# Moving preparations across stages of a graph-attention and feed-forward kernel

## The chip, the cores and the metric

The kernel runs on one core of a Trainium2 chip. The metric is the device time of one execution in microseconds (us), given as the median over several runs. The engines are PE (matrix multiply), DVE (vector), ACT (activation), POOL (GpSimd) and SP (which here only issues DMAs).

## The reference

`x` has 4096 rows of 256; `adj` is a 4096 x 4096 matrix of 0 and 1. Two layers run one after the other, each with an attention part and a feed-forward part, and each part is added to its input after a layer normalisation:

```python
x = x + gat4(layernorm(x), adj, W, a1, a2)           # 4 heads of 64
x = x + scan30(layernorm(x), ln_w, ln_b, W, b)       # 30 steps, below
x = x + gat4(gat4(layernorm(x), adj, W1, a1), adj, W2, a2)
x = x + top2_of_6_experts(layernorm(x))              # three products for each expert

def gat4(x, adj, W, a):                              # for each head
    h = x @ W; f1 = h @ a_src; f2 = h @ a_dst
    e = where(adj > 0, leaky_relu(f1[:, None] + f2[None, :], 0.2), -9e15)
    return elu(softmax(e) @ h)

def step(h):                                         # repeated 30 times
    h = h + 0.01 * tanh(h)
    h = h * sigmoid(h)
    h = layernorm(h) * ln_w + ln_b
    return h @ W.T + b
```

## The kernel before, in words

The rows are cut into 32 tiles of 128, and four tiles are a row group of 512; there are eight groups. Three attentions follow one another in the program, called g0 (first layer), g1 and g2 (second layer), with the feed-forward scan between g0 and g1 and the experts (routing and products, the last stage) after g2.

**An attention** has a front and a loop. The front goes over the eight row groups with two groups of lead: it loads rows, takes their layer statistics (`over_std`, L100 to L105, the last step a power on POOL), multiplies them with the weights and fills `vals` (the values, split in two parts of fp16) and the score columns. In g0 the front also begins to turn `adj` into packed masks (`make_piece`), which g1 and g2 load ready-made. The weight tensor of an attention has eight further columns, the products of W with the attention vectors; `make` computes them (products L148, reductions L149) and, where a layer normalisation precedes, subtracts the column means (PE L155, DVE L157), so that the normalisation needs no mean later. Before, the front of g0 makes the weights of all three attentions: its own at g == 0, those of g1 and g2 at g == 3 and g == 5 from the list `late`. All their loads stand at the start on ACT's DMA queue.

The loop has 128 units: four chunks of eight row tiles, in each the four heads, in each eight units of four column tiles. A unit is 64 matmuls into `acc` (L519). They are fed by four comparisons of scores for each unit (`st`: ACT L461 or DVE L459) and two DVE mask operations for each unit (`st` L567, `below` L573). At the end of a head the sums are closed while the next head runs: ACT copies the lower part (`lo`, L468), DVE adds it (`whole_sums`, L472, twice, which is also what frees `acc`), then come L482, L486, L489, a reciprocal, the product `o` (L494), on ACT the exponential `e` (L497), and in `finish` two more DVE operations (L622, L623) and the store (L624). The rows to be added, `old`, are loaded in `begin` (L615). `u`, one buffer, holds the sums; `e` has a tile of its own. After the last head, the closing has nothing beside it.

**The feed-forward scan** runs 30 steps over eight groups, 240 slots, in an order written out by hand (`slot`, under `manual_schedule`) with each slot holding stages of several groups: tanh (ACT L832) and the addition on POOL (L833) of group `at`; silu (ACT L821), its fp16 copy (L823) and a transposing DMA of group `at-2`; the transposes on PE (`tp`, L797) and their copy (`zT`, ACT L852) of `at-3`; the products (`po`, L869 and L872) of `at-4`; the result (`y`, DVE L805) of `at-5`. Each engine works in the order in which its instructions were issued. In the first slots the x1 rows of a group are also loaded, measured (bn_stats L676), rated (L684 to L688, with a power on POOL) and normalised (`init`, four ACT operations L695). POOL's addition waits by an explicit dependency for the last DVE instruction of the same slot[...].

Ahead of the slots stands the preparation of the scan's weights, L703 to L772: W transposed and multiplied by ln_w, its mean subtracted, a power-of-two scale derived from its size (`far`, `bits`, `scale`, `inv`), then `wT` and the fp16 pair `w16`. Loads of four groups of x1 stand on POOL's queue (`load(g, nc.gpsimd)`, L92).

**Buffers.** Row groups and pieces of adj are loaded into pools opened and closed by stage (`stream`). `numbers` (L961 to L963) fills constant tables by iota on POOL ahead of the last stage's routing.

Everything outside the hand-ordered slots is ordered by a scheduler from the program order and the dependencies.

Of the kernel before, what the change touches and what calls it, by code (L numbers as in the profile page):

```python
# [11 lines left out]
F32 = mybir.dt.float32  # L12
# [11 lines left out]
P = 128  # L24
# [22 lines left out]
def gnn_ffn_kernel(ctx: ExitStack, tc: tile.TileContext, a: dict, out: bass.AP):  # L47
# [19 lines left out]
    ones = const.tile([2 * H, P], F32, name="ones")  # L67
    nc.gpsimd.memset(ones, 1.0)
# [19 lines left out]
    stream = []  # L88

    def load_ahead(src, g, view=rows_of, queue=nc.sync):  # L90
        t = stream[-1].tile([P, G, C], F32, name="rows")
        queue.dma_start(t, view(src, g))  # L92
        ahead[g] = t
# [33 lines left out]
    def weights(tag, W, a_src, a_dst, norm):  # L127
# [4 lines left out]
        def load(pool):  # L132
            for k in range(KC):
                nc.scalar.dma_start(
                    w[:, k, :C].rearrange("p (h o) -> p h o", h=H),
                    W[:, k * P : (k + 1) * P, :].rearrange("h p o -> p h o"),
                )
            ab = pool.tile([P, 2, H, D], F32, name=f"{tag}_ab")
            nc.scalar.dma_start(ab[:, 0], bcast_rows(a_src))
            nc.scalar.dma_start(ab[:, 1], bcast_rows(a_dst))  # L140
            return ab

        def make(pool, small_ps, ab):
            prod = pool.tile([P, 2, H, D], F32, name="prod")
            for k in range(KC):
                wk = w[:, k, :C].rearrange("p (h o) -> p h o", h=H)
                for s in range(2):
                    nc.vector.tensor_tensor(prod[:, s], wk, ab[:, s], OP.mult)  # L148
                nc.vector.tensor_reduce(  # L149
                    w[:, k, C:].rearrange("p (s h) -> p s h", s=2), prod, axis=AX.X, op=OP.add  # L150
                )
            if norm:
                pt = small_ps()[:, : C + 2 * H]
                for k in range(KC):
                    nc.tensor.matmul(pt, mean, w[:, k, :], start=(k == 0), stop=(k == KC - 1))  # L155
                for k in range(KC):
                    nc.vector.tensor_tensor(w[:, k, :], w[:, k, :], pt, OP.subtract)  # L157

        return w, (load, make)

    def attention(tag, src, norm, w, others, chunks, first, ends, following):
# [7 lines left out]
        with ExitStack() as scope:  # L169
            lay = scope.enter_context(tc.tile_pool(name=f"{tag}_lay", bufs=1))  # L170
            vals = lay.tile([P, NT, H, 2, 2, DV], F16, name="vals")
            r = lay.tile([P, NT, H], F32, name="r")
            nf2 = lay.tile([P, NT, H], F32, name="nf2")
            hs = lay.tile([P, 1, H, DV], F32, name="hs")
            mask = [scope.enter_context(tc.tile_pool(name=f"{tag}_mask", bufs=4))]
# [20 lines left out]
            def load_piece(n):  # L196
# [3 lines left out]
                arow[n] = stream[-1].tile([P, 2, 8 * P], I32, name="adj")  # L200
# [32 lines left out]
            with ExitStack() as ps:  # L233
# [44 lines left out]
                def greatest():  # L278
# [8 lines left out]
                    nc.vector.tensor_scalar(dm, ident[: 2 * H, : 2 * H], fx, None, op0=OP.mult)  # L287
                    pt = small_ps()
                    nc.tensor.matmul(pt[:, : 2 * H], ones, dm, start=True, stop=True)
# [107 lines left out]
                late = [functools.partial(make, prep, small_ps, get(prep)) for get, make in others]  # L397
                for g in range(NG + 2):
# [10 lines left out]
                    if g == 0 and late:  # L409
                        late.pop(0)()  # L410
# [7 lines left out]
                    if g in (3, 5) and late:  # L418
                        late.pop(0)()
# [56 lines left out]
            def close(c, h, u):  # L476
# [17 lines left out]
                nc.vector.tensor_tensor(o[:, :nt], v[:, :nt, :D], z[:, :nt].to_broadcast([P, nt, D]), OP.mult)  # L494
                yield
                e = end.tile([P, CM, D], F32, name="e")
# [40 lines left out]
            with tc.manual_schedule(engines={mybir.EngineType.DVE, mybir.EngineType.Activation}):  # L537
# [3 lines left out]
                for at in range(len(units) + LAG):  # L541
# [43 lines left out]
                    if first:  # L585
# [8 lines left out]
                        if at == len(units) - 30:  # L594
                            store_mask(len(chunks) * PER // 4 - 1)
                    if following and at == len(units) - 2 * following[0]:
# [9 lines left out]
    def to_rows(dst, src=None):  # L606
# [5 lines left out]
        def begin(t, n, h, work):  # L612
            if src is not None:
                old = work.tile([P, 8, D], F32, name="old")
# [14 lines left out]
    w0, make = weights("g0", a["L0_gnn_W"], a["L0_gnn_a1"], a["L0_gnn_a2"], True)  # L629
    gw, makers = [], []  # L630
    for n in range(2):
        av = a[f"L1_gnn_a{n + 1}"]
        for got, to in zip(weights(f"g{n + 1}", a[f"L1_gnn_W{n + 1}"], av[:, :D], av[:, D:], not n), (gw, makers)):
            to.append(got)
    with tc.tile_pool(name="adj", bufs=2) as adjacency:
        stream.append(adjacency)
        attention("g0", x, True, w0, [make, *makers], [8, 8, 8, 8], True, to_rows(x1d, x), [])
    stream.append(ctx.enter_context(tc.tile_pool(name="stream", bufs=4)))

    with ExitStack() as scope:
        one = scope.enter_context(tc.tile_pool(name="f_one", bufs=1))
        wT = one.tile([P, C], F32, name="wT")  # L650
        w16 = one.tile([P, 2, C], F16, name="w16")
        scale = one.tile([P, 2], F32, name="scale")
        under = one.tile([P, 2, G], F32, name="under")
        eps = one.tile([P, 2], F32, name="eps")
        nc.gpsimd.memset(eps[:, :1], EPS)
        nc.gpsimd.memset(eps[:, 1:], EPS * 1e-4)
        bias = one.tile([P, C], F32, name="bias")
        last = one.tile([P, C], F32, name="last")
# [4 lines left out]
        x1 = {}  # L663

        def load(g, queue=nc.sync):
            if g not in ahead:
                load_ahead(x1d, g, queue=queue)
            x1[g] = ahead.pop(g)

        measured, rates = {}, {}  # L670

        def measure(g):
            st = small.tile([P, G, 6], F32, name="x_st")
# [708 lines left out]
```

## Time and profile before

| | us |
|---|---|
| median of three runs | 2999.38 (2998.97 to 3000.24) |
| the profiled execution | 3003.1 |
| its span | 3001.4 |
| g0: front, loop | to about 98, to 603.5 |
| feed-forward | to about 1578.6 |
| g1: front, loop | to 1645, to about 2126.6 |
| g2: front, loop | to about 2196, to about 2676.4 |
| routing and experts | to the end |

The profiled execution is one of its own, 3.7 us above the median of the others; its span is 1.7 us shorter than its time, which is what lies around the first and the last instruction. Over the span PE is busy 94%, DVE 91%, ACT 82% and POOL 39%; the clock granted to PE was 0.974 of full speed on average. Busy shares are averages over stages: each stage is read by itself.

### The profile page before, as it was taken

The numbers are of one execution on the slowest core, as the hardware profiler recorded it, in microseconds if no ns is written. First come the engines' busy times: TensorE is split into PE (matmuls) and PEld (weight loads), VectorE is DVE, ScalarE is ACT, GpSimd is POOL, SyncE is SP. The second block draws the span as 40 slices with busy tenths as digits, with TensorE's granted clock in tenths as the row PEclk, the third lists the DMA queues.
The fourth block names the chain that finished last, engine by engine and source line by source line (L and its number), as shares of the span: only waits on it lengthen the run. The fifth ranks groups of instructions, "written<-read, shape, count | busy, mean of one in ns | idle before, by whom it ended". The sixth has DMA issues, their size and how long they took to land. (4 is left out here: it accounts for less than half of the span.)

```text
span 3001.4 us, 82666 instructions
## 1 busy us (share of the span) xinstructions
PE 2812.5 (94%) x33923; PEld 2569.1 (86%) x33923; DVE 2737.4 (91%) x5766; ACT 2469.0 (82%) x3132; POOL 1161.5 (39%) x1080
## 2 busy tenths in 40 slices
PE   6899999969999999999998999999889999986996
PEld 5799999958888888888886999999789999975996
DVE  7999999989999999999998899999689999986775
ACT  5799999888888888888876999999699999963342
POOL 2000000079999999999982000000200000013663
PEclk9999999989999999999999999999999999997998
DMA  9998884153333333333353031221303132133253
GB/s 286 270 252 242 232 234 141 29 134 68 68 68 68 70 69 68 68 68 68 68 110 114 20 104 54 73 79 27 107 20 93 51 107 79 51 100 119 82 173 134
DMA packets 482899, 320.08 MB, mean 107 GB/s; under 512 B 416573, under 2 KB 443354, under 8 KB 476378
## 3 DMA queue, kind: packets, MB, share of 16 engines
q1 hardware_dynamic: 467698, 287.13, 35.8%
q0 software_dynamic: 7680, 21.51, 2.3%
q10 hardware_dynamic: 7144, 6.16, 0.7%
q8 instruction: 268, 4.39, 0.6%
q14 instruction: 109, 0.89, 0.1%
HBM read 183.00 MB, written 52.04 MB: 78 GB/s over the span
## 5 line engine op out<-in xcount | busy, mean ns | idle before, releaser
L519 PE MATMUL acc<-vals,st 128*128 128x130 f16 x12288 | 1434.6, 219 | 36.1 <-DVE u L472 27.5
L519 PE MATMUL acc<-vals,below 128*128 128x130 f16 x12288 | 1434.2, 221 | 12.4 <-DVE below L573 11.9
L461 ACT ACTIVATE st<-f1b,nf 128x1024 int8<-128x1024 f32 x1265 | 1334.6, 1143 | 32.7 <-PE acc L519 23.6
L519 PEld LDWEIGHTS <-below 128*128 128x128 fp8e4 x12288 | 1177.6, 96 | 48.8 <-issue 43.8
L519 PEld LDWEIGHTS <-st 128*128 128x128 fp8e4 x12288 | 1209.3, 98 | 10.0 <-DVE st L567 7.5
L869 PE MATMUL po<-wT,zT 128*128 128x256 f32 x1920 | 574.8, 381 | 4.7 <-ACT zT L852 3.4
L872 PE MATMUL po<-w,zT 128*128 128x256 f16 x3840 | 576.8, 273 | 0.0
L833 POOL TENSOR_TENSOR th<-th,y 128x1024 f32<-128x1024 f32 x240 | 567.2, 2363 | 21.7 <-ACT th L832 4.4
L872 PEld LDWEIGHTS <-zT 128*128 128x128 f16 x3840 | 376.2, 98 | 160.1 <-issue 0.6
L573 DVE TENSOR_TENSOR below<-m,st 128x1024 int32<-128x1024 int32 x384 | 470.0, 1224 | 32.7 <-DVE st L567 1.3
L567 DVE TENSOR_TENSOR st<-st,m 128x1024 int32<-128x1024 int32 x384 | 467.5, 1217 | 1.1 <-ACT st L461 0.9
L805 DVE SCALAR_TENSOR_TENSOR y<-po,z_rs,bias 128x256 f32<-128x256 f32 x928 | 384.5, 477 | 2.1 <-PE tp L797 0.7
L845 DVE BATCH_NORM_STATS2 z_st<-z 128x6 f32<-128x256 f32 x960 | 335.9, 413 | 0.0
L869 PEld LDWEIGHTS po<-wT,zT 128*128 128x128 f32 x1920 | 290.4, 191 | 14.0 <-ACT zT L852 5.8
L821 ACT ACTIVATE z<-th 128x1024 f32<-128x1024 f32 x240 | 251.8, 1049 | 15.2 <-POOL th L833 14.9
L105 POOL TENSOR_TENSOR ln_rstd<-ln_rstd,mhalf 128x4 f32<-128x4 f32 x24 | 31.7, 1321 | 590.9 <-ACT acc L1035 491.8
L832 ACT ACTIVATE th<-y 128x1024 f32<-128x1024 f32 x240 | 250.1, 1042 | 0.1
L856 POOL TENSOR_TENSOR z_rs<-z_rs,mhalf 128x4 f32<-128x4 f32 x240 | 244.1, 1017 | 3.1 <-ACT z_rs L855 3.1
L852 ACT COPY zT<-tp 128x512 f32<-128x512 f32 x240 | 140.5, 585 | 90.8 <-PE tp L797 89.5
L459 DVE TENSOR_SCALAR st<-f1b,nf 128x1024 int8<-128x1024 f32 x271 | 201.2, 743 | 7.7 <-PE acc L519 7.7
L436 POOL MEMSET hs<- 128x4 f32 x3 | 0.3, 101 | 497.7 <-DVE u L489 491.1
L824 DVE SCALAR_TENSOR_TENSOR z<-z,scale,z 128x512 f16<-128x512 f32 x240 | 178.4, 743 | 4.9 <-ACT z L823 4.9
(253 smaller groups left out, 2961.2 us busy)
## 6 DMA issues: line engine op xcount, KB each, us to landing
adj<-in_adj_dram SPq DMA_DIRECT2D x64, 1024.0 KB
m<-edges SPq DMA_DIRECT2D x32, 1024.0 KB
f1b<-fd SPq DMA_DIRECT2D x48, 512.0 KB
edges<-m SPq DMA_DIRECT2D x16, 1024.0 KB
y<-yd SPq DMA_DIRECT2D x16, 512.0 KB
ew<-in_L_ffn_expert_w_dram SPq DMA_DIRECT2D x18, 256.0 KB
t<-in_x_dram SPq DMA_DIRECT2D x8, 512.0 KB
old<-in_x_dram SPq DMA_DIRECT2D x16, 256.0 KB
```

The lines of the kernel that those rows point to most:

```text
L461: nc.scalar.activation(out, f1, AF.Sign, bias=f2, scale=-1.0)
L519: nc.tensor.matmul(acc[:, i, cols], masked[part][:, at_i // TR, s, rows], v[:, cols], start=(j == 0 and part == 0), stop=(j == NT - 1 and ...
L567: nc.vector.tensor_tensor(above, above, whole, OP.bitwise_and)
L573: nc.vector.tensor_tensor(below, whole, above, OP.bitwise_xor)
L805: nc.vector.scalar_tensor_tensor(t[:, r, :] if end else y[:, g * G + r, :], po[:, r, :], rstd[:, r : r + 1], t[:, r, :] if end else bias, ...
L821: nc.scalar.activation(z, th.pop(u), AF.Silu, scale=0.01)
L832: nc.scalar.activation(th[at], y[:, g * G : (g + 1) * G, :], AF.Tanh, scale=0.01)
L833: ins = nc.gpsimd.tensor_tensor(th[at], th[at], y[:, g * G : (g + 1) * G, :], OP.add)
L845: nc.vector.bn_stats(st[:, r, :], z[:, r, :])
L856: nc.gpsimd.tensor_tensor(rs[u], rs[u], mhalf, OP.pow)
L869: nc.tensor.matmul(po[:, r, :], src[:, r * P : (r + 1) * P], wT, start=True, stop=False)
L872: nc.tensor.matmul(po[:, r, :], src16[:, part * G + r, :], w16[:, other, :], start=False, stop=(part == 1 and other == 1),)
```

## The change

The scan's weights are made in g0's front, at g == 2, instead of after its loop; some of the operations go from DVE to ACT or POOL. The products of g1's weights go into g0's last chunk and those of g2's into g1's last chunk, at units counted from the end (`side`); the subtraction of the mean (`centre`) of g1's goes to the start of g1's front. The first four groups of x1 are loaded by SP and measured in g0's last chunk, and rated there; `init` normalises in place, one slot earlier. Groups 4 to 7 get tiles of their own. Input rows and pieces of adj share one ring of four buffers for the whole kernel. `e` is written into the half of `u` that is no longer needed; `old` shares the two buffers of `lo`. The iota of the large table is cut in four with one shared integer buffer. The first POOL addition of the scan waits for `o` of the last head. The diff, cut to its core:

```diff
+    closed = []
+    ring = keep.tile([P, 4, G, C], F32, name="ring")
+    turns = [0]
 
     def load_ahead(src, g, view=rows_of, queue=nc.sync):
-        t = stream[-1].tile([P, G, C], F32, name="rows")
+        t = ring[:, turns[0] % 4]
+        turns[0] += 1
...
-        def load(pool):
+        def load(space, queue):
+            ab = space[:, : 2 * C].rearrange("p (s h d) -> p s h d", s=2, h=H)
             for k in range(KC):
-                nc.scalar.dma_start(
+                queue.dma_start(
                     w[:, k, :C].rearrange("p (h o) -> p h o", h=H),
                     W[:, k * P : (k + 1) * P, :].rearrange("h p o -> p h o"),
                 )
-            ab = pool.tile([P, 2, H, D], F32, name=f"{tag}_ab")
-            nc.scalar.dma_start(ab[:, 0], bcast_rows(a_src))
-            nc.scalar.dma_start(ab[:, 1], bcast_rows(a_dst))
-            return ab
-
-        def make(pool, small_ps, ab):
-            prod = pool.tile([P, 2, H, D], F32, name="prod")
+            queue.dma_start(ab[:, 0], bcast_rows(a_src))
+            queue.dma_start(ab[:, 1], bcast_rows(a_dst))
+
+        def make(space, k):
+            ab, prod = (
+                space[:, i * 2 * C : (i + 1) * 2 * C].rearrange("p (s h d) -> p s h d", s=2, h=H) for i in range(2)
+            )
+            wk = w[:, k, :C].rearrange("p (h o) -> p h o", h=H)
+            for s in range(2):
+                nc.vector.tensor_tensor(prod[:, s], wk, ab[:, s], OP.mult)
+            nc.vector.tensor_reduce(w[:, k, C:].rearrange("p (s h) -> p s h", s=2), prod, axis=AX.X, op=OP.add)
+
+        def centre(small_ps):
+            pt = small_ps()[:, : C + 2 * H]
             for k in range(KC):
-                wk = w[:, k, :C].rearrange("p (h o) -> p h o", h=H)
-                for s in range(2):
-                    nc.vector.tensor_tensor(prod[:, s], wk, ab[:, s], OP.mult)
-                nc.vector.tensor_reduce(
-                    w[:, k, C:].rearrange("p (s h) -> p s h", s=2), prod, axis=AX.X, op=OP.add
-                )
-            if norm:
-                pt = small_ps()[:, : C + 2 * H]
-                for k in range(KC):
-                    nc.tensor.matmul(pt, mean, w[:, k, :], start=(k == 0), stop=(k == KC - 1))
-                for k in range(KC):
-                    nc.vector.tensor_tensor(w[:, k, :], w[:, k, :], pt, OP.subtract)
-
-        return w, (load, make)
-
-    def attention(tag, src, norm, w, others, chunks, first, ends, following):
+                nc.tensor.matmul(pt, mean, w[:, k, :], start=(k == 0), stop=(k == KC - 1))
+            for k in range(KC):
+                nc.vector.tensor_tensor(w[:, k, :], w[:, k, :], pt, OP.subtract)
+
+        return w, (load, make, centre)
...
+                arow[n] = ring[:, 2 * (n % 2) : 2 * (n % 2) + 2].rearrange("p s r c -> p s (r c)").bitcast(I32)
...
-                late = [functools.partial(make, prep, small_ps, get(prep)) for get, make in others]
+                late = (front(prep, small_ps) if front else None) or []
...
-                    if g == 0 and late:
+                    if g in (0, 2) and late:
...
-                    if g in (3, 5) and late:
-                        late.pop(0)()
...
+                closed[:] = [
+                    nc.vector.tensor_tensor(o[:, :nt], v[:, :nt, :D], z[:, :nt].to_broadcast([P, nt, D]), OP.mult)
+                ]
...
-                e = end.tile([P, CM, D], F32, name="e")
+                e = u[:, :, 1, :D]
...
+                    if len(units) - at in side:
+                        side[len(units) - at]()
...
-                old = work.tile([P, 8, D], F32, name="old")
+                old = work.tile([P, 4, 2, DV], F32, name="old", tag="lo", bufs=2)
...
+    def begin_weights(n):
+        load, _, _ = layers[n][1]
+        load(ring[:, 3].rearrange("p r c -> p (r c)"), nc.sync)
+
+    def make_weights(n, k):
+        layers[n][1][1](ring[:, 3].rearrange("p r c -> p (r c)"), k)
...
+    def load_ffn():
+        ln = w16[: 2 * KC, 0, :].bitcast(F32)
+        nc.scalar.dma_start(ln[:KC], a["L0_ffn_ln_w"].rearrange("(k p) -> k p", p=P))
+        nc.scalar.dma_start(ln[KC:], a["L0_ffn_ln_b"].rearrange("(k p) -> k p", p=P))
+        wr = wT, last
+        for k in range(KC):
+            nc.scalar.dma_start(wr[k], a["L0_ffn_W"][k * P : (k + 1) * P, :])
+        nc.scalar.dma_start(bias, bcast_rows(a["L0_ffn_b"]))
+        return ln, wr
+
+    def make_ffn(prep, small_ps, loaded):
+        ln, wr = loaded
+        ps = small_ps()
+        nc.tensor.transpose(ps[:, : 2 * KC], ln, ident[: 2 * KC, : 2 * KC])
+        lnT = prep.tile([P, 2 * KC], F32, name="lnT")
+        nc.vector.tensor_scalar(lnT, ps[:, : 2 * KC], 100.0, None, op0=OP.mult)
+        ps = small_ps().rearrange("p (k c) -> p k c", k=KC)
+        for k in range(KC):
+            for o in range(KC):
+                nc.tensor.transpose(ps[:, k, o * P : (o + 1) * P], wr[o][:, k * P : (k + 1) * P], ident)
+        raw = prep.tile([P, KC, C], F32, name="raw", tag="g0_ab")
+        nc.scalar.copy(raw, ps)
...
+        nc.vector.scalar_tensor_tensor(bias, bias, 100.0, ps, op0=OP.mult, op1=OP.add)
+        nc.gpsimd.tensor_scalar(last, bias, -100.0, 0.01, op0=OP.add, op1=OP.mult)
+        for k in range(KC):
+            nc.scalar.activation(raw[:, k, :], raw[:, k, :], AF.Copy, scale=lnT[:, k : k + 1])
...
+        sq = prep.tile([P, KC, C], F32, name="sq")
+        nc.scalar.activation(sq, raw, AF.Square)
...
+        nc.gpsimd.tensor_tensor(far[:, 1:2], far[:, 0:1], mhalf[:, :1], OP.pow)
+        nc.gpsimd.tensor_tensor(far[:, 1:2], far[:, 1:2], far[:, 0:1], OP.mult)
...
+        nc.gpsimd.tensor_scalar(under[:, 1, :], under[:, 0, :], 0.01, None, op0=OP.mult)
+        nc.vector.tensor_scalar(wT, raw[:, 0, :], scale[:, :1], scale[:, 1:], op0=OP.mult, op1=OP.mult)
+        nc.scalar.activation(w16[:, 0, :], raw[:, 1, :], AF.Copy, scale=scale[:, 1:])
...
+    def init(g):
+        rs, nm = rates.pop(g)
+        for r in range(G):
+            nc.scalar.activation(
+                x1[g][:, r, :], x1[g][:, r, :], AF.Identity, scale=rs[:, r : r + 1], bias=nm[:, r : r + 1]
+            )
...
+    def front(prep, small_ps):
+        load, make, centre = layers[0][1]
+        space = prep.tile([P, 4 * C], F32, name="g0_ab")
+        load(space, nc.scalar)
+        loaded = load_ffn()
+
+        def make_first():
+            for k in range(KC):
+                make(space, k)
+            centre(small_ps)
+
+        return [make_first, lambda: make_ffn(prep, small_ps, loaded)]
+
+    side = {
+        31: [(begin_weights, 1)],
+        28: [(load, g) for g in range(3)],
+        26: [(make_weights, 1, 0)],
+        22: [(make_weights, 1, 1)],
+        20: [(load, 3)],
+        14: [(measure, 0)],
+        8: [(measure, 1)],
+        4: [(rate, 0), (rate, 1), (measure, 2)],
+        1: [(measure, 3), (init, 0), (init, 1), (rate, 2), (rate, 3)],
+    }
+    attention(
+        "g0",
+        x,
+        True,
+        w0,
+        front,
+        [8, 8, 8, 8],
+        True,
+        to_rows(x1d, x),
+        [],
+        {k: functools.partial(many, *v) for k, v in side.items()},
...
-        for g in range(4):
-            load(g, nc.gpsimd)
...
-            for g in range(3):
-                measure(g)
-                if g < 2:
-                    rate(g)
-            init(0)
...
+        hold = scope.enter_context(tc.tile_pool(name="f_hold", bufs=NG - NG // 2))
+
+        def load_apart(src, g):
+            x1[g] = hold.tile([P, G, C], F32, name="x1")
+            nc.sync.dma_start(x1[g], rows_of(src, g))
+
+        for g in range(4, NG):
+            load_apart(x1d, g)
...
-            if 0 < at and at + 3 < NG:
-                load(at + 3)
...
+                was = x1.pop(at) if at < NG else y[:, g * G : (g + 1) * G, :]
+                nc.scalar.activation(th[at], was, AF.Tanh, scale=0.01)
+                ins = nc.gpsimd.tensor_tensor(th[at], th[at], was, OP.add)
+                if not at:
+                    lower = closed[0]
...
-            if at + 2 < NG:
-                rate(at + 2)
-            if at + 1 < NG:
-                init(at + 1)
-            if at + 3 < NG:
-                measure(at + 3)
+            if 4 <= at + 3 < NG:
+                rate(at + 3)
+            if 2 <= at + 2 < NG:
+                init(at + 2)
+            if 4 <= at + 4 < NG:
+                measure(at + 4)
...
+    def centre_weights(prep, small_ps):
+        layers[1][1][2](small_ps)
...
+        for k, v in {24: (begin_weights, 2), 14: (make_weights, 2, 0), 10: (make_weights, 2, 1)}.items()
...
+            parts = 4 if math.prod(shape) > 1024 else 1
+            shape[0] //= parts
+            for i in range(parts):
+                ti = rone.tile([P, *shape], I32, name=f"{name}_i", tag="ints")
+                nc.gpsimd.iota(
+                    ti,
+                    pattern=[list(x) for x in zip([s for s, _ in pattern], shape)],
+                    base=base + i * shape[0] * pattern[0][0],
+                    channel_multiplier=step,
+                )
+                nc.gpsimd.tensor_copy(tf[:, i * shape[0] : (i + 1) * shape[0]], ti)
```

## The prediction

> **What bounds the kernel now.** I read the profile page first, then busy time by stretches, then the ACT and PE timelines where PE is idle, then the waits of the loops and the chain at the last stage. Columns of the stretches: PE, PEld, DVE, ACT, POOL busy us, granted clock, DMA share, GB/s.
>
> ```profile
> 50.00:100.00 50.00, 32.81 (x150) 25.41 (x148) 47.09 (x87) 34.58 (x53) 16.36 (x24) 0.86 0.96 298
> ...
> 540.00:600.00 60.00, 59.40 (x1028) 59.15 (x1026) 56.87 (x72) 49.98 (x51) 0.00 (x0) 1.00 0.10 23
> 600.00:610.00 10.00, 5.06 (x68) 4.50 (x66) 9.72 (x33) 2.32 (x5) 1.54 (x4) 0.93 0.23 54
> 610.00:620.00 10.00, 5.52 (x12) 2.78 (x10) 5.31 (x11) 7.23 (x14) 6.21 (x9) 0.50 0.88 263
> 620.00:630.00 10.00, 1.11 (x4) 0.71 (x4) 9.20 (x35) 8.11 (x13) 6.54 (x6) 0.50 0.53 165
> 630.00:640.00 10.00, 8.52 (x45) 6.32 (x46) 8.09 (x36) 9.94 (x20) 9.45 (x11) 0.70 0.57 157
> ...
> 650.00:750.00 100.00, 98.90 (x707) 80.75 (x706) 98.51 (x330) 89.74 (x134) 94.39 (x77) 1.00 0.41 74
> ```
>
> The reader should see three regimes: the first front is DVE's (47.09 of 50); the loop's end and the feed-forward are PE's (59.40 of 60, 98.90 of 100), with DVE only 5% behind; and from 603.5, the last attention matmul, to about 650 nothing is full. That seam is what the change attacks. On ACT's timeline it reads:
>
> ```profile
> 611.64 2.07 ACT L695 ACTIVATE y<-rows,x_nm,x_rs 128x256 f32<-128x256 f32 x4 [2.33 <-POOL x_nm L688]
> ...
> 621.38 1.28 ACT L821 ACT_TABLE_LOAD   x1
> 622.68 1.06 ACT L821 ACTIVATE z<-th 128x1024 f32<-128x1024 f32 x1
> 625.60 0.72 ACT L823 ACTIVATE z<-z,scale 128x512 f16<-128x512 f32 x1 [1.86 <-DVE inv L763]
> ```
>
> and on PE's:
>
> ```profile
> 632.59 1.22 PE L869 MATMUL po<-wT,zT 128*128 128x256 f32 x2 [1.06 <-ACT zT L852]
> ...
> 654.29 0.70 PE L869 MATMUL po<-wT,zT 128*128 128x256 f32 x2 [1.10 <-ACT zT L852]
> ```
>
> The first normalised group is ready only at 613.7, the first silu at 622.7, its fp16 copy waits for the weights' scale until 625.6, the first product is at 632.59; the fifth is at 654.29, and from there a slot takes 3.89 us.
>
> **The change, part by part** (line numbers of before).
>
> *The seam.* I replay it with before's durations. Gone from the tail: the measures and rates of groups 0 to 2 (26 bn_stats of 0.41 us), the whole weight chain L703 to L772, and four DMA issues on ACT, of which L703 (0.50) stands ahead of the last `lo`. The last head's closing (L472 to L494) then runs without measures between: `o` ends near 607.95 instead of 608.64. tanh(0) follows the last `lo` at 604.2 (before: 613.74). POOL's first add now waits for `o` (the added dependency): 608.0 to 610.35; behind it on POOL stand only the adds of the next slots. ACT: init(2), tanh(1), the closing's Exp at 608.6 and init(3) fill it to 611.25; table load 1.28; silu(0) at 612.55; zT(0), formerly 9.3 us after silu(0) with 1.9 of that waiting for the scale, at about 620.4; first product 621.0, which is 11.6 earlier. The slots that still carry an init take ACT's 5.47 us (as 643.5 to 649.0 before), one slot fewer than before: the fourth product comes at 638.0. PE-bound start, product time less slots of 3.89: before 654.29-4x3.89=638.7, after 638.0-3x3.89=626.3. **Gain 12.4** (9 to 14: lower if the ring's reloads or the inits hold a slot).
>
> *The weight chain in the front.* Its DVE share is 4.1 us (bias .42, subtracts .75, two reduces .83, wT .38, w16 .46, small ones), plus 2.3 on ACT, which is 34.58 of 50 busy, and a few PE and POOL pieces; wr is now two DMAs, five issues on ACT in all. Leaving the front: g1's DVE work (four products 0.37, two reductions 0.68, subtracts 0.76) 3.6 and g2's 2.9, with eight ACT DMA issues. Net DVE -2.3 in a stage where DVE is 94% busy. One other row is worth seeing, from the groups of the seam:
>
> ```profile
> L747 DVE TENSOR_TENSOR far<-far 128x1 f32<-128x1 f32 x1 | 2.3, 2296 | 0.7 <-POOL far L746 0.7
> ```
>
> A one-element DVE product took 2.30 us while POOL was in its 2.36 us add; it moves to POOL and to a place without such an add. **Gain 2** (-1 to 4: DVE is in order, and a link that comes late from ACT or POOL stalls it).
>
> *Chunk 3 of the first loop.* In come two product steps of 1.35 us and three measures of 1.65 on DVE (the fourth falls behind the last matmul), and loads on SP (W, then x1 groups; the queue has only 0.10 DMA share to serve); POOL's four row loads leave at no price, POOL being idle. DVE's unit is 3.43 us against PE's 3.63, so it wins back 0.2 per unit and has 2 to 3 us of lead: one insertion of 1.35 to 1.65 fits, two close together need seven units each. **Cost 1** (0 to 3).
>
> *The store wait.* `e` now lies in `u`, so the next head's first whole-sum (L472) waits until the head's store has landed. Each of the 45 boundaries inside the loops gets this wait on DVE; behind it stand masks and `below` for PE, and `acc` is freed by it. Waits of PE on that row are now, in the first loop and then in the second:
>
> ```profile
> PE acc L519 <- DVE u L472: 18.4, 16, 3.0
> ```
> ```profile
> PE acc L519 <- DVE u L472: 4.6, 15, 0.3
> ```
>
> Store issue to landing in this trace, against issue to next whole-sum: in the second loop 2.55 against 3.8 to 4.5 us, except that every fourth store, which meets a mask load, takes 5.16 to 5.39; in the third 3.0, and 5.1 to 5.2 likewise; in the first 3.1 to 5.4 against 3.5 to 5.9. Overshoots: first loop 6.5 in eight places, second 4.6 in four, third 3.9 in three. Each has 0.73 of cover (the second whole-sum waits that long for ACT's `lo` anyway): second 1.6, third 1.7; for the first I take 1.7, since `old`, which shared the queue 0.7 us ahead of the store, is now issued much earlier. The rule that bears on it: the Trainium skill, "DMA: Bandwidth & Descriptors", section "Anatomy of one DMA — SWDGE (gpsimd) path", fits one DMA of GpSimd's path as about 2.0 us fixed plus bytes over 436 GB/s. For 256 KB that is an estimate of 2.6 us, which the undisturbed 2.55 of these SP stores matches, and it would cost the wait at nothing, since the shortest gap is 3.47. But the fourth stores measure twice that. I take the trace: **cost 5** (0 to 12); by the rule the forecast would be 5 us lower. `old` in `lo`'s two buffers only makes SP wait elsewhere; its data is needed microseconds later: nothing, bound by one more such wait, within the 12.
>
> *Second front and loop.* `centre` (subtracts 0.76 on DVE, 1.05 on PE) moves from the DVE-bound first front into g1's, which is a dependency chain: **cost 1** (0 to 1.5). g2's products, 2x1.35 on DVE, have the loop's gaps of about 1.4 per head: **0.3** (0 to 1). Sharing the input ring keeps the same number of buffers for the rows: nothing, at most the latency of one 512 KB load (6.1 us) if one is late, which is rival 2. `mean` for `ones` changes an operand, not an instruction: nothing.
>
> *Last stage.* Chain, start and length:
>
> ```profile
> 2684.00 4.14 DMA x3d<-e
> ...
> 2688.86 2.39 POOL along_i L961 x2
> ...
> 2695.59 0.99 POOL ln_rstd L105
> ```
>
> The last group's rstd queues behind 6.7 us of number making on POOL. In the new order only about two of the four quarter tables stand ahead of it, by the same rows about 4.6 us; PE idles 1.94 for it. **Gain 1.5** (-1 to 2, six extra instructions being the risk).
>
> Sum: 12.4+2+1.5-1-5-1-0.3 = **8.6 us less**. The profiled execution took 3003.1 (span 3001.4 and 1.7 around it): 2994.5 for it. It stands 3.7 above the median of the runs, 2999.38, against which the result is measured, so 2999.4-8.6 = **2990.8**.
>
> **The rivals.**
> 1. *The store wait eats everything: slower.* Place: L472 at the head boundaries. Without it the change gains 13.6; it is level at 0.30 us net per boundary over 45, and slower by 6 at 0.44. If moved DMAs make every store land like the fourth ones (mean overshoot 1.2, 0.5 after cover), 45x0.5=22 us, time 3008. For it: eight of fifteen overshoot already in the first loop. Against: the undisturbed 2.55.
> 2. *The seam gains half.* ACT is 9.94 of 10 busy at 630 to 650 with inits; if a ring reload for groups 4 to 7, or POOL's wait for `o`, holds the slots back, the gain is 6 and the time 2997.
> 3. *Chunk 3 becomes DVE's.* At 56.87 of 60, the 7.7 us of insertions pay half: 4 instead of 1, 2994.
> 4. *Waits hidden, front better.* Store wait 0 to 1, front 4: 2984.
> That the change does not do what it says: the front has no room and its 4.1 us lengthen it. This is the end of the front's range and adds at most 3.
>
> **How the numbers follow.** Forecast 0.56, rival 1 0.10, 2 0.13, 3 0.08, 4 0.13. 0.2%, 6 us, is what a measurement of this kernel can tell from no change, so faster needs under 2993.4. The forecast case reaches it in five of six (0.47), rival 4 always (0.13), rivals 2 and 3 together 0.05: 0.65. Slower, over 3005.4: most of rival 1, 0.09. The rest, 0.26, is the same. Range: rival 4's end with a seam of 14 gives 2983; upward rival 2's time with a store wait of 8 gives 3000.
>
> **What would show it.** Right: the first feed-forward product (L869) comes 17 or 18 us after the last attention matmul, where it now comes 29 after; the first silu about 9 us after that matmul; PE's waits on the whole-sum row grow by 1 to 3 us in each loop; the last group's rstd about 2 us after the third quarter table starts. Wrong: the waits on that row over 5 us per loop (rival 1); the distance still over 23 (rival 2); PE under 58.5 of 60 in the loop's last 60 us (rival 3); the first `acc` matmul later than in before.

## The result and the profile after

The changed kernel takes 2992.36 us (median of 22 runs) where the kernel before, measured with it on the same chip, takes 2997.68 (22 runs): a ratio of 0.9982 with a 95% interval of 0.9975 to 0.9988, that is 5.3 us less (3.6 to 7.5). The forecast was 8.6 less: more than this interval allows, and inside the forecast's range. The profiled execution took 2996.19, its span is 2994.5, against 3003.1 and 3001.4 before. Cut at the first and last attention matmuls and at the feed-forward's products, the two traces differ by 6.9 us (by this cut the fronts of g1 and g2 end at 1640.4 and 2190.6 in the trace before, some 5 us earlier than the table of times before has them):

| stretch, us | before | after | difference | forecast |
|---|---|---|---|---|
| start to the first `acc` matmul | 96.8 | 94.7 | -2.2 | -2 |
| loop of g0 | 506.7 | 507.7 | +1.0 | +2.7 |
| last `acc` to the ninth feed-forward product | 66.6 | 56.1 | -10.4 | -12.4 |
| ninth to last product | 908.3 | 908.3 | 0 | 0 |
| front of g1 | 62.1 | 60.4 | -1.7 | +1 |
| loop of g1 | 486.2 | 489.7 | +3.5 | +1.9 |
| front of g2 | 64.0 | 65.0 | +1.0 | 0 |
| loop of g2 | 485.7 | 491.4 | +5.7 | +1.7 |
| last stage | 325.0 | 321.2 | -3.8 | -1.5 |

The traces of the experiments below show how far such differences can be trusted, since several kernels share the code of a stretch. The first front takes 95.2 to 96.8 us in the three kernels that have it as before and 92.5 to 94.7 in the nine that have it as here. The loops of g1 and g2 take 489.7 to 492.5 and 488.0 to 491.4 in the seven kernels that write `e` into `u` as here. The stretch from the last `acc` to the ninth product takes 55.4 to 57.0 in all kernels that keep both early preparations out of it. A single difference of one or two microseconds says little outside that stretch.

The stretches around the seam, with the same columns as before (PE, PEld, DVE, ACT, POOL busy us, granted clock, DMA share, GB/s):

```profile
50.00:100.00 50.00, 34.48 (x165) 27.24 (x166) 47.29 (x80) 35.05 (x54) 14.64 (x25) 0.83 0.96 290
...
540.00:600.00 60.00, 57.43 (x987) 56.91 (x987) 58.64 (x92) 52.84 (x61) 6.39 (x9) 1.00 0.08 18
600.00:610.00 10.00, 2.32 (x41) 2.14 (x38) 9.12 (x24) 8.05 (x15) 3.79 (x5) 0.76 0.16 37
610.00:620.00 10.00, 2.23 (x8) 1.43 (x8) 5.54 (x11) 9.40 (x15) 8.37 (x9) 0.50 0.70 206
620.00:630.00 10.00, 8.62 (x45) 6.23 (x46) 9.37 (x38) 7.74 (x17) 7.18 (x7) 0.72 1.09 206
```

The front is still DVE's, at 47.29 of 50. PE's return, which stood in the row 630 to 640, now stands at 620 to 630. In the rows of ACT and of PE the table load, the silu and the first product come 11.3 to 12.5 us earlier, and the fp16 copy (L871) no longer waits for the scale:

```profile
610.09 1.28 ACT L869 ACT_TABLE_LOAD   x1
611.39 1.06 ACT L869 ACTIVATE z<-th 128x1024 f32<-128x1024 f32 x1
612.48 0.72 ACT L871 ACTIVATE z<-z,scale 128x512 f16<-128x512 f32 x1
```
```profile
620.09 1.22 PE L920 MATMUL po<-wT,zT 128*128 128x256 f32 x2 [1.05 <-ACT zT L903]
...
638.76 0.70 PE L920 MATMUL po<-wT,zT 128*128 128x256 f32 x2 [1.10 <-ACT zT L903]
```

The waits on the whole-sum (engine and line, what it waited for: total, times, longest) have grown, and a new kind has come, the store. First the second loop, then the third:

```profile
DVE u L472 <- DMA h1d<-u: 10.9, 4, 5.5
PE acc L521 <- DVE u L472: 7.7, 15, 1.8
```
```profile
PE acc L521 <- DVE u L472: 7.6, 14, 2.4
DVE u L472 <- DMA x3d<-u: 6.2, 3, 3.3
```

In both loops PE waited 4.6 us on that row before. Of DVE's 10.9 us, 5.5 belong to the last head of the loop, whose matmuls are then all but done. In the last stage, POOL's work is interleaved so that two quarter tables and the third one's iota stand ahead of the last group's rstd. The loop of g2 ends at 2673.3 here, at 2676.4 before, so the rstd comes 17.0 us behind it instead of 19.1:

```profile
2689.72 0.65 POOL L1024 IOTA along_i<- 128x512 int32 x1
2690.34 1.05 POOL L106 TENSOR_TENSOR ln_rstd<-ln_rstd,mhalf 128x4 f32<-128x4 f32 x1
```

### The profile page after: what moved, and what is told of

Same layout as the page of the kernel before. It is cut to its first block, busy times and chain, and to the rows that moved or that the text cites. A ratio compares the mean times of both kernels' runs of the same rounds, so it can differ in the third digit from the quotient of the medians.

```text
span 2994.5 us, 82658 instructions
## 1 busy us (share of the span) xinstructions
PE 2805.8 (94%) x33923; PEld 2567.1 (86%) x33923; DVE 2735.7 (91%) x5756; ACT 2472.4 (83%) x3137; POOL 1160.0 (39%) x1085
## 5 line engine op out<-in xcount | busy, mean ns | idle before, releaser
L521 PE MATMUL acc<-vals,below 128*128 128x130 f16 x12288 | 1434.9, 221 | 12.0 <-DVE below L575 11.4
L882 POOL TENSOR_TENSOR th<-th,y 128x1024 f32<-128x1024 f32 x232 | 548.5, 2364 | 14.8 <-issue 0.2
L869 ACT ACTIVATE z<-th 128x1024 f32<-128x1024 f32 x240 | 251.8, 1049 | 14.6 <-POOL th L882 14.4
L881 ACT ACTIVATE th<-y 128x1024 f32<-128x1024 f32 x232 | 241.7, 1042 | 0.0
L757 POOL TENSOR_TENSOR x_rs<-x_rs,mhalf 128x4 f32<-128x4 f32 x8 | 10.2, 1280 | 505.4 <-ACT x_rs L756 505.4
```

Source lines behind the costliest of these rows:

```text
L521: nc.tensor.matmul(acc[:, i, cols], masked[part][:, at_i // TR, s, rows], v[:, cols], start=(j == 0 and part == 0), stop=(j == NT - 1 and ...
L869: nc.scalar.activation(z, th.pop(u), AF.Silu, scale=0.01)
L881: nc.scalar.activation(th[at], was, AF.Tanh, scale=0.01)
L882: ins = nc.gpsimd.tensor_tensor(th[at], th[at], was, OP.add)
```

## The experiments

Ratios are against the kernel before, measured on the same chip at the same time, with 95% intervals. The level differs from one such session to another (before: 2997.7 us with the changed kernel, 3010 to 3016 with the experiments, where the last stage of all kernels takes 333 to 340 us), so times of different sessions are compared by their ratios, and stretches by the traces. The loop of g0 varies most: 502.6 to 511.4 us over the kernels that have its measures where they were or where the change puts them, so a microsecond there says nothing.

**1. The store wait taken out.** The third and second loop get their own tile for `e` back; in g0's loop there is no room for it.

```diff
-                e = u[:, :, 1, :D]
+                e = u[:, :, 1, :D] if first else end.tile([P, CM, D], F32, name="e")
```

> The changed kernel, but e has a tile of its own again in the second and the third attention loop (in the first it stays in u). Theory (the store wait): in the changed kernel DVE waited 10.9 us and 6.2 us for the store in these two loops, and PE's idle time grew by 3.2 us in each; without the wait the loops go from 489.7 and 491.5 us back to 486 to 488 and 485.5 to 486.5, and the time is 5 to 9 us below the changed kernel. Rival (the wait only takes the place of another; the loops are longer because of the two product steps, the clock, or loads that moved): the loops lose under 2 us together, the time under 2.

Measured: 0.9964 (0.9952 to 0.9976), that is 5.4 us below the changed kernel's ratio. The loop of g1 takes 488.0 us, that of g2 486.1: 1.7 and 5.3 less than in the changed kernel's trace. Over all traces the seven kernels with `e` in `u` average 490.8 and 489.4 us in these loops, the four with a tile of its own 488.0 and 486.4: 2.8 and 2.9 less. The third loop's row is back where it was before the change:

```profile
PE acc L521 <- DVE u L472: 4.5, 15, 0.3
```

The second loop keeps 5.9 on this row, its longest 1.7; the rest of its cost is another (experiment 4).

**2. The store wait put in, alone.** The opposite edit, in the kernel before, in all three loops.

```diff
-                e = end.tile([P, CM, D], F32, name="e")
+                e = u[:, :, 1, :D]
```

> The kernel before with one edit: e is written into u, in all three attentions, so the next head's first whole-sum waits for the store. Theory: the wait alone costs 3 to 5 us in the second and the third loop each and 1 to 4 in the first, 7 to 13 us in all, about 3007. The prediction's size for it, 5 us, would give 3003. Rival (the wait is covered): within 2 us of before.

Measured: 1.0038 (1.0024 to 1.0051), 11.4 us slower (7.2 to 15.4). The loops of g1 and g2 take 487.6 and 489.0, which is 1.5 and 3.3 more; g0's has about 4 us more PE idle time than before. The total and the third loop are as the theory had them; the second loop's share is smaller than its 3 to 5. First loop, then third:

```profile
PE acc L519 <- DVE u L472: 23.2, 15, 2.7
DVE u L472 <- DMA x1d<-u: 9.0, 9, 1.8
```
```profile
PE acc L519 <- DVE u L472: 7.5, 15, 1.8
DVE u L472 <- DMA x3d<-u: 5.9, 3, 2.7
```

Nine boundaries of g0's loop wait here; in the changed kernel only two do, for 1.7 us together. There `old` is issued much earlier, and the stores of the first loop land in 2.55 to 4.6 us instead of 3.1 to 5.4, as the prediction had it.

**3. The four-part table alone.** In the kernel before, `numbers` is replaced by the new one.

> The kernel before with one edit: the large constant table ahead of the routing is made in four parts with one shared integer buffer. Theory: the last group's rstd on POOL starts 2.1 us earlier after the third loop's last matmul (17.0 instead of 19.1 us) and the last stage gets shorter by 1.5 to 3.8 us. Rival (the 3.8 us that the last stage lost in the changed kernel come from elsewhere, the order of loads or chance): the rstd moves but the stage changes by under 1 us.

Measured: 0.9985 (0.9978 to 0.9991), 4.5 us faster. Its last stage takes 336.6 us, and those of experiments 1 and 4, with the new tables too, 337.7 and 336.2; that of experiment 2, on the same chip and with the old tables, 339.9. The rstd of the last group comes 17.1 us after the loop, as in the changed kernel. The 2.1 us of POOL's queue are shown; why the stage gains up to 1.7 more than that is not.

**4. The third attention's two product steps apart**, with `e` in its own tile. In the changed kernel they stand in the third and the seventh unit of the same head (a head has eight); here each stands in the third unit of a head, two heads apart.

```diff
-        for k, v in {24: (begin_weights, 2), 14: (make_weights, 2, 0), 10: (make_weights, 2, 1)}.items()
+        for k, v in {70: (begin_weights, 2), 54: (make_weights, 2, 0), 38: (make_weights, 2, 1)}.items()
```

> The changed kernel with e in a tile of its own in the second and third loop, and the third attention's weight products moved from units 114 and 118 of the second loop to units 74 and 90, their loads to unit 58. Theory: one PE gap of 1.75 us in the second loop comes from the two product steps of 2.7 us of DVE within four units of a head's end; 16 units apart in the middle of a head they cost nothing: 1 to 2 us below the run with e of its own alone, the second loop at 485.5 to 486.5. Rival: the gap is the store's or chance, and nothing more is gained.

Measured: 0.9972 (0.9960 to 0.9984), not to be told from experiment 1. In the trace the loop of g1 takes 487.2 instead of 488.0, and PE's idle time in it, without the gap of 4.8 us near its start, is 5.2 instead of 6.0 us, where the kernel before has 4.5. A PE gap of 1.66 us, which the three other kernels with `e` in its own tile all have near this loop's end, is gone. The second step near the head's end costs a microsecond or less, under what the time can show.

**5. The feed-forward's weights computed behind the loop again.** The list that the front gets ends with `make_first`; `make_ffn` is called after `load_apart`, with pools of its own.

> The changed kernel, but the feed-forward's weights are computed behind the first attention loop again (their loads stay at the start). Theory: the chain, with its POOL powers and DVE steps behind POOL's additions, again holds the first fp16 copy and gives back 3 to 7 us of the seam (17.8 us from the last attention matmul to the first product), while the first front gets shorter by 2 to 4 us: 1 to 4 us slower than the changed kernel in all. Rival (the chain was hidden behind the measures and inits before, its place is worth nothing): the seam within 1 us, and the time not slower.

Measured: 0.9994 (0.9985 to 1.0003), 3.6 us above the changed kernel. The first front takes 89.8 us, 4.8 less than in the changed kernel's trace (in experiment 8, with the same front, 91.6; the nine kernels with the weights in it average 93.6); the ninth product comes 61.0 us behind the last attention matmul, 4.8 later. The fp16 copy waits behind the weight scale on ACT again:

```profile
618.46 0.51 ACT L731 ACTIVATE w<-raw,scale 128x256 f16<-128x256 f32 x1 [2.06 <-DVE scale L719]
618.88 0.71 ACT L877 ACTIVATE z<-z,scale 128x512 f16<-128x512 f32 x1
```

So early weights are worth 4.8 us in the seam (3.6 by experiment 8 against 7) and cost some 3 in the DVE-bound front by the averages (4.8 by this one pair of traces). The net is small, up to 2 us by the traces and 3.6 by the ratios, whose intervals overlap.

**6. The x1 measures moved back in program order.** Their entries leave `side` and stand ahead of the slots.

> The changed kernel, but groups 0 to 3 of x1 are measured and rated behind the first loop again (their loads stay in its last chunk, the weights stay early). Theory: DVE's measures stand before the last whole-sums or the inits wait for POOL's powers as before, 5 to 9 us of the seam come back; the last chunk of the first loop loses at most 1 to 3 us of PE idle time; 4 to 8 us slower than the changed kernel. Rival (the early weights alone made the gain): the seam within 2 us.

Measured: 1.0011 (1.0003 to 1.0019), 8.7 us above the changed kernel, but not for the reason expected. The seam is as short as before this edit (17.2 us to the first product). The scheduler put the measures where their loads allow, from 470.7 us on, those of groups 4 and 5 at 544 to 548:

```profile
L748 DVE BATCH_NORM_STATS2 x_st<-ring x16: 397/420/428, 470.7 to 536.4; 128x6 f32<-128x256 f32 x16
```

and PE stood at three head boundaries for 4.30 (2.49 at the same one in the changed kernel), 3.31 and 3.20 us:

```profile
480.42 0.27 PE L521 MATMUL acc<-vals,st 128*128 128x130 f16 x1 [4.30 <-DVE u L472]
```

At the first and the last of these the bn_stats stand straight ahead of the whole-sum on DVE (eight of them in the 4.1 us before 548.2); at 515 DVE itself waits 2.54 for ACT's `lo`, which stands behind four init operations on ACT, 2.06 us from 511.25 on. The loop of g0 took 517.1 us, 9.4 more, 7.2 of it as PE idle time. At two boundaries this is rival 3 of the prediction, DVE as the bound of chunk 3; in the changed kernel the measures stand at chosen units near the end instead, one of which has the same fault (see “Chunk 3” below).

**7. The measures held behind the last head's `o`.** As experiment 6, with an explicit dependency of the measures of groups 0 to 3.

> The changed kernel with groups 0 to 3 of x1 measured behind the last head's o, held there by an explicit dependency (in the run with the measures moved back in program order alone, the scheduler put them into the last chunk all the same, earlier and in one heap, where PE lost 7 us). Theory: the seam grows by 4 to 7 us (four measures of 1.65 on DVE, then rate on POOL with its powers, then the inits on ACT, all ahead of the first addition), the first loop keeps its length or loses up to 1 us. Rival: the measures were never on the path, the seam grows by under 2 us.

Measured: 1.0017 (1.0011 to 1.0024), 10.5 us above the changed kernel. Both theories were too low: the ninth product comes at 68.0, 11.8 us later than in the changed kernel and 1.4 later than in the kernel before, where part of the measures ran ahead of the last whole-sums. Now the chain measure, rate on POOL, init on ACT stands whole in the seam; the table load waits behind the fourth init:

```profile
609.69 1.09 ACT L773 ACTIVATE ring<-ring,x_nm,x_rs 128x256 f32<-128x256 f32 x2 [1.75 <-POOL x_nm L767]
...
617.59 2.07 ACT L773 ACTIVATE ring<-ring,x_nm,x_rs 128x256 f32<-128x256 f32 x4 [1.47 <-POOL x_nm L767]
...
622.78 1.28 ACT L874 ACT_TABLE_LOAD   x1
```

**8. Both behind the loop.** Experiments 5 and 7 together.

> The run with the measures behind o and the feed-forward's weights computed behind the loop as well. Theory: the two parts overlap in the seam, since one is DVE and ACT work and the other a chain with waits: seam and first slots together 10 to 14 us longer than in the changed kernel, at least as long as in the kernel before, and the front 4 to 5 us shorter; 5 to 9 us slower than the changed kernel. Rival: they hide each other, no longer than the longer of the two alone.

Measured: 1.0030 (1.0019 to 1.0041), 14.4 us above the changed kernel. The ninth product comes at 71.6 us: 15.4 later, where the two alone make 4.8 and 11.8. They add but for 1.2, where the theory had them overlap and the whole cost 5 to 9.

**9. POOL's first addition behind the head's last DVE operation.** The forecast had the fourth product 34.5 us behind the last attention matmul; it came at 36.4. In the trace of the changed kernel, DVE is held three times on the way:

```profile
608.15 2.42 DVE L627 SCALAR_TENSOR_TENSOR u<-u,old 128x512 f32<-128x512 f32 x1 [0.70 <-ACT u L499]
610.60 2.72 DVE L628 SCALAR_TENSOR_TENSOR u<-u 128x512 f32<-128x512 f32 x1
...
620.12 1.40 DVE L748 BATCH_NORM_STATS2 x_st<-x 128x6 f32<-128x256 f32 x4 [4.54 <-DMA x<-x1d]
```

The two last operations of the head run beside POOL's additions and take 2.42 and 2.72 us; so the store is late, and the loads of groups 6 and 7 behind it. The edit moves the entry of `closed` from `o` to L628.

> The changed kernel with one edit: POOL's first addition waits for the head's last DVE operation (L628) instead of for o (L495). In the changed kernel L627 and L628 took 2.42 and 2.72 us beside POOL's two additions, where 0.69 is usual, so the last store came at 613.35, and the loads of groups 6 and 7, which wait for it, held DVE 4.54 us at the measure of group 6; the second product came 7.46 us after the first. Theory: the store goes 3 to 4 us earlier, DVE's wait for group 6 falls under 1.5 us, the addition itself starts 1.9 us later and delays the first product by at most 0.6; the fourth product, 36.4 us behind the last attention matmul, comes at 34 to 35: 1.5 to 2.5 us faster. Rival (the slots are paced by ACT's inits whatever DVE does): the fourth product moves by under 0.5 us.

Measured: 0.9984 (0.9977 to 0.9992). The theory fell: the two operations take 0.69 us each and the store goes 3.8 us earlier,

```profile
605.32 0.69 DVE L625 SCALAR_TENSOR_TENSOR u<-u,old 128x512 f32<-128x512 f32 x1 [0.70 <-ACT u L497]
606.04 0.69 DVE L626 SCALAR_TENSOR_TENSOR u<-u 128x512 f32<-128x512 f32 x1
...
617.25 1.41 DVE L746 BATCH_NORM_STATS2 x_st<-x 128x6 f32<-128x256 f32 x4 [3.50 <-DMA x<-x1d]
```

but the first product comes 1.7 us later, the fourth stays at 36.4, and the ratio is that of the changed kernel. The loads of groups 6 and 7 still stood on SP behind a reload of the ring that waited for POOL's second addition.

**10. Experiment 9 with `e` in its own tile.**

> Both edits that take cost out of the changed kernel: e in a tile of its own in the second and third loop, and POOL's first addition behind the head's last DVE operation. Theory: the gains add, 7 to 9 us below the changed kernel, 12 to 15 below the kernel before. Rival: they do not add, and it is within 2 us of the run with e of its own (0.9964 of before).

Measured: 0.9957 (0.9944 to 0.9970), 7.5 us below the changed kernel, as the theory had it, but within the interval of experiment 1: with experiment 9 alone worth nothing, the runs don't show that anything was added to `e`'s own tile.

**11. The reloads behind the loads of groups 6 and 7**, on top of experiment 9: the loads of the ring that are wanted for the last step depend on the last measure.

> The run with POOL's first addition behind the head's last DVE operation, and in addition the reloads of groups 0 to 3 of x1 (wanted only for the last step) held behind the measure of group 7. In the run with the addition alone the last store went out 3.8 us earlier, but one reload waited 2.67 us on SP's queue for POOL's second addition, ahead of the loads of groups 6 and 7, and DVE still waited 3.50 us for group 6; the fourth product stayed at 36.4 us behind the last attention matmul. Theory: that queue was the second gate; now the loads go at about 10 us instead of 12.6, DVE's wait falls to about 1 us, the fourth product comes at 34 to 35.5, and the time is 1 to 2.5 us below the run with the addition alone. Rival: ACT's and POOL's own chain (inits, powers, additions) paces the slots, and the fourth product stays within 0.5 us of 36.4.

Measured: 0.9987 (0.9979 to 0.9995), no gain against experiment 9. DVE's wait for group 6 is gone, and the fourth product comes at 35.7, which is 0.8 earlier: nearer to the rival. What remains is the POOL and ACT chain:

```profile
615.62 1.48 POOL L765 TENSOR_TENSOR x_rs<-x_rs,mhalf 128x4 f32<-128x4 f32 x1
```
```profile
617.73 2.08 ACT L774 ACTIVATE x<-x,x_nm,x_rs 128x256 f32<-128x256 f32 x4 [1.40 <-POOL x_nm L768]
```

The power for group 4's rate queues behind two additions (4.65 us), and ACT's next init, with the slot's silu behind it, waits for it. No run here takes that wait out.

**12. All three edits.**

> The same two edits with e in a tile of its own in the second and third loop: the version meant to be best. Theory: 0.9957 of before, less another 0.0005: 0.995. Rival: within 1.5 us of the run with e of its own and the addition behind the close.

Measured: 0.9961 (0.9946 to 0.9976). The four kernels with `e` of its own lie at 0.9957 to 0.9972, the three that keep it in `u` and move nothing back at 0.9982 to 0.9987. The mean of the four is about 5.5 us below the changed kernel, though three of their intervals overlap with its, two of them by 0.0001; among the four the runs show no best.

## Why the prediction was right, and where its terms were off

The direction and the range were right, and so was most of the mechanism; the total agrees in part by luck, because errors of both signs cancel: in the two traces the terms that came out worse than forecast add up to 8.6 us, those that came out better to 6.9.

- *The seam: right in kind, 2.0 too large.* The first product comes 17.8 us after the last attention matmul, as forecast (17 or 18; rival 2's sign was over 23), but the fourth at 36.4 instead of 34.5. The prediction took 5.47 us for each slot with an init (three of them behind 621.0 make 637.4, not the 638.0 it went on with); the first took 7.46. Of this, 0.8 is a load queue (group 6, experiment 11); behind it the trace shows POOL's power waiting for two additions, which is read from the trace and not tested. One premise fell as well: the last head's closing doesn't run free of measures, since those of groups 3 to 5 stand ahead of the last whole-sums until 603.0, and `o` ends 5.1 us behind the last attention matmul, as before, not 4.5. (The 26 bn_stats counted for groups 0 to 2 are twelve in the program, four to a group; no term of the sum is worked out from that count.) Experiments 5 to 8 divide the seam: the measures in the loop carry most of it (11.8 us when undone), the weights 4.8.
- *The front: right, -2.2 against -2.* Experiments 5 and 8 show its two halves: without the later attentions' weights the front is 5.5 us shorter by the averages (7.0 in one pair of traces), against 6.5 of DVE work summed, and the feed-forward's give back 2.9 (4.8), against 4.1.
- *Chunk 3: the place decides.* The forecast of a small cost held, but rival 3's sign came: PE is busy 57.6 of the loop's last 60 us, under the 58.5 that was named, against 59.4 before. Nearly all of it is one gap at the boundary of the last head, where the second measure stands on DVE between ACT's `lo` and the whole-sum that frees `acc`:

```profile
569.65 1.40 DVE L748 BATCH_NORM_STATS2 x_st<-ring 128x6 f32<-128x256 f32 x4
...
571.88 0.69 DVE L472 TENSOR_TENSOR u<-acc,lo 128x520 f32<-128x520 f32 x1
```
```profile
572.62 0.22 PE L521 MATMUL acc<-vals,st 128*128 128x130 f16 x1 [2.31 <-DVE u L472]
```

  All eight kernels that measure at this unit have this gap of 2.31 us and 57.6 of 60; the three that measure elsewhere (experiments 6 to 8) have 0.30 there, as before, and 59.4 to 59.7. So the cost is about 2 us at one boundary, not a DVE-bound chunk: the whole loop is +1.0, inside its scatter. Moving this measure a few units away was not run. Experiment 6 shows what such DVE work can cost in other places.
- *The store wait: the step that was most under-sized.* In loops 2 and 3 it was put at 3.3 us; taking it out gains 7.0 in one pair of traces and 5.7 by the averages of experiment 1. The prediction counted each overshoot against the landings of before, and forgot two things. A store's landing isn't a constant: the one issued at 2423.66, 1.3 us behind a mask load, took 6.95 us, where the worst of the third loop had been 5.19. And PE doesn't always lose just the gap, 2.39 us there: the clock granted to it fell for a while after. Start, end and length, then the five engines, the clock and DMA:

```profile
2428.00:2432.00 4.00, 1.61 (x25) 1.49 (x23) 1.29 (x2) 4.00 (x5) 0.00 (x0) 0.91 0.04 13
2432.00:2436.00 4.00, 4.00 (x50) 4.00 (x48) 4.00 (x5) 2.58 (x3) 0.00 (x0) 0.67 0.31 70
```

  The row 2432 to 2436 has 50 matmuls where undisturbed 4 us of before have 73, about 1.3 us of work. The estimate of 2.6 us from the fit in the Trainium skill (“DMA: Bandwidth & Descriptors”, section “Anatomy of one DMA — SWDGE (gpsimd) path”), which would have made the wait free, holds for undisturbed stores here too (2.55 to 2.6 in most heads); the trace was the right side to take, for the reason given. Rival 1, every boundary late, did not come: stores near the mask loads overshoot, the others do not. PE's waits on the whole-sum row grew by 3.5, 3.1 and 3.0 us in the three loops, at or just over the upper end of the 1 to 3 that was named; some 2 of the 3.5 belong to the measure above.
- *`centre` in the second front: wrong sign.* The first product of g1's front does come 1.65 us later, but the fourth group's comes 1.4 us earlier, and the front is shorter in all kernels that keep this part. The rows are loaded through the ring there; that this is the cause was not tested.
- *The g2 products: 0.3 forecast, up to 0.8 shown* (experiment 4).
- *The last stage: right in place, too small.* The rstd moved by 2.1 us against the 2 taken from the order, though it starts 0.6 us after the third quarter table and not 2; the stage gained 3.8, and with the tables alone 3.3 (experiment 3 against 2).

## What to carry to other kernels

When a tile is folded into another to save memory, list the last reader of each part: if it is a store, the next writer pays the store's landing, and this has a long tail wherever big loads share the queue. A preparation moved to an earlier stage is free only if the engine it uses there isn't that stage's bound; here 4.1 us of DVE work moved into a DVE-bound front cost some 3 of the 4.8 that it gained in the seam. In a loop with 5% of slack on the second engine, small extra work is cheap away from the point where the first engine waits for it and dear straight ahead of that point; a scheduler that goes by dependencies may well put it there, and so may a hand-picked unit: the second measure at the last head's boundary costs 2 us.

## What was not expected of the hardware

- Two DVE operations on 128x512 took 2.42 and 2.72 us beside POOL's additions on 128x1024, 0.69 each without them (experiment 9).
- A PE gap of 2.39 us was followed by 4 us at a granted clock of 0.67, so that stall cost more than its length. Another of 2.31 us (at 572.62 in the changed kernel) was followed by 4 us at 1.00; what makes the difference the runs don't show.
- A store of 256 KB landed in 2.55 us undisturbed and in up to 6.95 us behind a mask load on the same queue.
- The level of the same program differed between sessions by 13 to 18 us in 3000, a good part of it in the last stage (325.0 us in the first trace, 339.9 in another with the same code there); why is open.
